# A decoder layer: queries' and keys' kept copies laid out so that one transfer with a repeating source fetches 64 rows, in place of four of 16

## The chip, the cores and the metric

The kernel runs on one core of one Trainium2 chip. A core has five engines with an instruction queue each: TensorE (PE, matrix products; its weight loads are listed as PEld), VectorE (DVE), ScalarE (ACT), GpSimd (POOL) and SyncE (SP), which here only issues DMA transfers. Sixteen DMA engines move data between HBM and the on-chip memory. The metric is the device time of one execution in microseconds (us); lower is better. Several executions are timed and the median is given; one more is recorded by the hardware profiler.

## The reference

One pre-norm decoder layer in float32, for x of shape (4, 1024, 256) and a context of shape (4, 64, 256): layer norm and self-attention with 16 heads of 16 columns, layer norm and cross-attention to the 64 context rows, and a feed-forward block with ternary weights. Shortened:

```python
def attention(x, W_qkv, b_qkv, W_out, b_out):          # B=4, N=1024, E=256, 16 heads, d=16
    q, k, v = split(x @ W_qkv + b_qkv)
    energy = einsum('bqhe,bkhe->bqhk', q, k)           # not scaled before the softmax
    attn = softmax(energy, axis=-1) / sqrt(E)
    return einsum('bihv,bvhd->bihd', attn, v).reshape(B, N, E) @ W_out + b_out

x = x + attention(layernorm(x), ...)
x = x + cross_attention(layernorm(x), ctx, ...)        # 64 context rows, 16 heads, scores / sqrt(16)
x = x + ffn(x)                                         # layernorm(gelu(x @ ternary(W_fc).T)) @ ternary(W_proj).T

def ternary(W):                                        # absmean
    gamma = mean(abs(W)) + 1e-6
    return sign(W / gamma) * minimum(round(abs(W / gamma)), 1)
```

The self-attention scores are large, since they are not scaled and the biases are, so they are computed from a high and a low part of each factor.

## The kernel before, in words

The four sequences are batches b = 0 to 3; the 16 heads of a batch are four groups g of four heads. One group of one batch is a unit, u = 4b + g, and the kernel goes through the 16 units in order.

*Projection.* `project(b, c)` (L348) computes queries and keys of half of the heads of a batch (c = 0: groups 0 and 1; c = 1: groups 2 and 3), in four pieces of 512 columns (tokens): q half 0, k half 0, k half 1, q half 1. A piece is two products of 256 columns on PE (L363); ACT writes each product's high part, rounded to fp32r, into a buffer `hl` (L366), and DVE the low part, which is the product minus its high part (L367). A piece's `hl` has 128 rows (features) by 2 parts by 512 columns. One transfer (L372) then writes it to scratch tensors in HBM, `kept_q` or `kept_k`, of shape (2, 128, 1024): part, feature, token. There are two buffers of the kind `hl`, and other short-lived tiles use them as well (`bv_wide`, `neg`, `lnb_wide`).

*Fetching.* `fetch(u)` (L375) reads the unit's queries and keys back from the scratch tensors. A unit is two pairs of heads, and each pair has a tile q and a tile k of 128 rows by 1024 columns: 64 rows for either head n of the pair. These 64 rows are four blocks of the head's 16 features: q has the parts (high, high, low, low), k has (high, low, high, low), so that one product over 64 rows sums the four products of parts. Each block of 16 rows is a transfer of its own, 64 KB, so a pair needs 16 transfers and a unit 32. Unit 0's are cut into two halves of the columns as well, which makes 64, and eight of those are issued by POOL (`aside`). The tiles q and k have four buffers each, so two units' worth.

*The main loop.* Each unit has 16 steps: two halves of the queries by eight blocks of 128 keys. A step computes the scores of both pairs (PE: a product of k and q, and one of the selection matrix `sel` with the transposed maxima `mT`, which subtracts each row's maximum), their exponentials (ACT, L906: four a step, 128 by 512), and the weighted sum with the values (`weigh`, PE into `ps_acc`). The maxima come from a pass of their own that runs ahead of the scores by 19 of its pieces: `maxima(u)` (L423) has 32 pieces, each two products of q and k (`ps_ring<-k,q`) and two maximum reductions on DVE (`mx`, L445, about 0.68 us each). So a unit's k is first used about at step 6 of the unit before. A planner with due times (`due`, `later`, `aside`) puts other work into the steps: layer norm `ln1(b)`, the projections and values of coming batches, the context's side, the cross-attention `post(b)` of batches that are done, and from unit 13 on the ternary weights. All of it shares a ring of seven PSUM banks; an eighth bank holds the weighted sums.

*Order.* PE's and SP's instructions keep the order of the program. Those of DVE, ACT and POOL are placed when the kernel is built, by a scheduler that models durations, except where one is pinned; an engine then runs them strictly in that order. SP issues its transfers in order, too, and each transfer uses one of eight semaphores in turn: it waits for the landing of the one eight before it.

*What else SP issues near the fetches.* Unit 1's fetch is followed by the load of batch 1's rows (`x<-in_x`, 1 MB), by the context's weights and biases (`late_loads`, L776, which has the loads of `wo` and `xwo`: 32 KB each, 32 rows of 1 KB, read as 2 x 16 rows). Unit 2's fetch, in the first two steps of unit 1, is followed by batch 2's rows. Unit 14's and unit 15's fetches are followed by the loads of the raw weights of the feed-forward block (`raw<-in_wfc`, `raw<-in_wproj`, 1 MB each); DVE first sums their absolute values (`part<-raw`, L735). Layer norm begins with statistics of the loaded rows on DVE (`bn<-x`, L241).

In before's fetch, one head's 64 rows are read by

```python
for i, part in enumerate(order):                      # (0, 0, 1, 1) for q, (0, 1, 0, 1) for k
    r, f = 64 * n + 16 * i, f0 + 16 * n
    issue(out=t[r : r + 16, cols].bitcast(F32), in_=kept[part, f : f + 16, cols])
```

Of the kernel before, what the change touches and what calls it, by code (L numbers as in the profile page):

```python
# [9 lines left out]
F32 = mybir.dt.float32  # L10
# [7 lines left out]
B, S, E = 4, 1024, 256  # L18
H, D = 16, 16
SK = 64  # L20
HID = 1024
P = 128
# [8 lines left out]
def decoder_layer(ctx, tc, a, out):  # L31
# [15 lines left out]
    nc = tc.nc  # L47
# [14 lines left out]
    def dma(**kwargs):  # L62
        ordered(nc.sync.dma_start(**kwargs))
# [38 lines left out]
    for name in ("wq", "wk"):  # L102
# [5 lines left out]
        t = const.tile([P, E // P, H, D], F32, name=name)  # L108
# [4 lines left out]
    for name in ("bq", "bk"):  # L113

        t = const.tile([P, 2], F32, name=f"{name}_c")
        for g in range(NG):
            r = 64 * (g % 2)
            dma(
                out=t[r : r + 64, g // 2 : g // 2 + 1],
                in_=a[name].rearrange("(j e) g -> g j e", e=32)[g, :, 1 : 1 + D],  # L120
# [35 lines left out]
    dram = main_stack.enter_context(tc.tile_pool(name="dram", bufs=1, space=DRAM))  # L156
# [4 lines left out]
    for i in range(3):  # L161
        t = (const if i else main).tile([P, NT, VW], F32, tag=f"v_sb{i}", name=f"v_sb{i}")
# [28 lines left out]
    def bank():  # L191
        return ps[state["banks"]]()
# [4 lines left out]
    def product(out, terms, start=True, stop=True):  # L197

        n = len(terms)
        strips = [slice(32 * j, 32 * j + 32) for j in range(4)] if state["split"] else [slice(0, P)]  # L200
        for i, (lhsT, rhs) in enumerate(terms):
            for r in strips:
                matmul(
                    out[r, :], lhsT=lhsT[:, r], rhs=rhs, start=start and i == 0,
                    stop=stop and i == n - 1,
                )
# [122 lines left out]
    xnT_of, qk_of, split_of, m_of, pieces_of = {}, {}, {}, {}, {}  # L329

    def ln1(b):
        mv = main.tile([P, NT, 2], F32, tag="mv1", name="mv1", bufs=2)
        rs = main.tile([P, NT], F32, tag="rs1", name="rs1", bufs=2)
        xnT_of[b] = xnT = main.tile([P, 2, S], F32, tag="xnT", name="xnT")
        n = NT if state["split"] else NT // 2
        for i0 in range(0, NT, n):
            for i in range(i0, i0 + n, 2):
                yield "free"
                ln_stats(main, mv, [(i + k, b * NT + i + k) for k in range(2)])
            yield "free"  # L340
            ln_rstd(main, rs[:, i0 : i0 + n], mv[:, i0 : i0 + n, :])
            for i in range(i0, i0 + n, 4):
                yield "free"
                xn = ln_normalised(post_pool, mv, rs, i, b * NT + i, 4)
                yield "rows"
                ln_transposed(xnT[:, :, i * P : (i + 4) * P], xn)

    def project(b, c):  # L348

        split_of[b, c] = [  # L350
            dram.tile([2, P, S], F32, tag=f"kept_{name}", name=f"kept_{name}", bufs=6) for name in "qk"
        ]
        first = (b, c) == (0, 0)

        for side, half in ((0, 0), (1, 0), (1, 1), (0, 1)):
            w, bias = (wq, wk)[side], bqk[("bq", "bk")[side]][:, c : c + 1]
            hl = main.tile([P, 2, 512], F32, tag="exp" if first and half else "hl", name="hl", bufs=4 if first and half else 2)
            width = 256 if state["split"] else 512
            for i0 in range(0, 512, width):
                yield "cols+"  # L360
                cols, part = slice(half * 512 + i0, half * 512 + i0 + width), slice(i0, i0 + width)
                pq = bank()[:, 0:width]
                product(  # L363
                    pq, [(w[:, i, c * P : (c + 1) * P], xnT_of[b][:, i, cols]) for i in range(2)]
                )
                nc.scalar.activation(hl[:, 0, part].bitcast(F32R), pq, AF.Identity, bias=bias)  # L366
                nc.vector.scalar_tensor_tensor(  # L367
                    hl[:, 1, part], pq, bias, hl[:, 0, part], ALU.add, ALU.subtract
                )
            cols = slice(half * 512, (half + 1) * 512)  # L370
            issue = nc.scalar.dma_start if first and (side or half) else dma
            issue(out=split_of[b, c][side][:, :, cols].rearrange("l p t -> p l t"), in_=hl)  # L372
            pieces_of[b, c] = pieces_of.get((b, c), 0) + 1

    def fetch(u):  # L375

        b, g = divmod(u, NG)
        pairs = qk_of[u] = []
        rest = []
        for pair in range(2):  # L380
            q = main.tile([P, S], F32R, tag="q", name="q", bufs=4)
            k = main.tile([P, S], F32R, tag="k", name="k", bufs=4)
            pairs.append((q, k))
            kept_q, kept_k = split_of[b, g // 2]
            f0 = 64 * (g % 2) + 32 * pair

            def parts(t, kept, order, n, cols, issue, f0=f0):
                for i, part in enumerate(order):
                    r, f = 64 * n + 16 * i, f0 + 16 * n
                    issue(out=t[r : r + 16, cols].bitcast(F32), in_=kept[part, f : f + 16, cols])  # L390

            if u:
                halves = (slice(0, S),)
            else:
                halves = (slice(0, 512), slice(512, S))
            for n in range(2):
                parts(q, kept_q, (0, 0, 1, 1), n, halves[0], dma)
            for cols in halves:
                for n in range(2):

                    aside = u == 0 and pair == 1 and n == 0
                    parts(k, kept_k, (0, 1, 0, 1), n, cols, nc.gpsimd.dma_start if aside else dma)
            for n in range(2):
                for cols in halves[1:]:
                    rest.append((parts, q, kept_q, (0, 0, 1, 1), n, cols, dma))
            if pair:
                for f, *args in rest:
                    f(*args)
            yield
# [278 lines left out]
    due, later, aside = Line(), Line(), Line()  # L688
# [141 lines left out]


    first, parts = ln1(0), project(0, 0)
    for _ in range(10):
        next(first)
# [3 lines left out]
    run(parts)  # L838
    state.update(split=True, pinned=False)
    run(fetch(0))  # L840

    sel_f = post_pool.tile([P, 2, P], F32, tag="xn", name="sel_f", bufs=2)
    nc.gpsimd.memset(sel_f, 0.0)
    sel = main.tile([P, 2, P], F32R, name="sel")
    for pair in range(2):

        for n in range(2):
            c = 64 * n + 2 * pair
# [17 lines left out]


    parts = project(0, 1)
    for _ in range(5):
        next(parts)  # L870
# [11 lines left out]
    run(turning.popleft())  # L882
    due.credit = 0.0
    run(fetch(1))
    load_x(1)
    loading = late_loads()
# [22 lines left out]
    for u in range(NU):  # L909
        b, g = divmod(u, NG)  # L910
# [4 lines left out]
        if g == 0:  # L915
            if b == 0:
                later.add(context(), 6)
                later.add(value_bias(), 1)

            for n in ((1, 2), (), (3,), ())[b]:  # L920
                if n > 2:
                    load_x(n)
                due.add(ln1(n), 2)
                due.add(project(n, 0), 8)
                due.add(values(n), 8)
                if n == 1:
                    due.add(project(n, 1), 8)
            if b % 2:

                due.add(project(b // 2 + 2, 1), 8)  # L930
            if b == B - 1:
                load_x(0, view=x_kept, slot=1)
# [4 lines left out]
        for step in range(2 * NT):  # L937
# [3 lines left out]
            if step < 2 and 0 < u < NU - 1:  # L941
                if step == 0:
                    while pieces_of.get(divmod((u + 1) // 2, NG // 2)) != 4:
                        due.step()
                    fetching = fetch(u + 1)
                next(fetching)
# [152 lines left out]
    halves = 2 * B  # L1099
# [3 lines left out]
    tag = later.tag  # L1103
    while tag is not None or narrows:
        turn += 1
        if tag is not None and turn % 5 in (0, 2):
            exps += "Exp" in tag
            tag = next(last, None)
            continue
        sources = []  # L1110
        if wides:
            i = halves - len(wides)
# [72 lines left out]
```

## Time and profile before

| | before |
|---|---|
| median of 3 executions | 1333.93 us (1332.51 to 1334.63) |
| the profiled execution | 1333.76 us |
| its span, first to last instruction | 1331.7 us |
| TensorE clock granted, mean | 0.977 |
| PE busy | 1251.0 us, 94% |
| DVE busy | 1041.5 us, 78% |
| ACT busy | 841.5 us, 63% |
| POOL busy | 98.3 us, 7% |
| transfers q<-kept_q on SP | 240 of 64 KB, and those of unit 0 |
| transfers k<-kept_k on SP | 240 of 64 KB, and those of unit 0 |
| bytes by the queue that SP feeds | 68.73 MB, 16.4% of 16 engines' span |

Busy times are shares of the whole span. In a timeline each line has the start, the length, the engine, the source line, the operation, what it writes and reads, how many instructions the line stands for, and in brackets how long the engine stood idle before it and what ended that. "DMA k<-kept_k" in the chain or the waits means that something waited for that transfer to land. A row of a window has the length, the busy time of PE, PEld, DVE, ACT and POOL with the number of instructions, PE's granted clock as a share of full speed, the DMA engines' mean busy share and the data rate in GB/s.

### The profile page before, as it was taken

The numbers are of one execution on the slowest core, as the hardware profiler recorded it, in microseconds if no ns is written. First come the engines' busy times: TensorE is split into PE (matmuls) and PEld (weight loads), VectorE is DVE, ScalarE is ACT, GpSimd is POOL, SyncE is SP. The second block draws the span as 40 slices with busy tenths as digits, with TensorE's granted clock in tenths as the row PEclk, the third lists the DMA queues.
The fourth block names the chain that finished last, engine by engine and source line by source line (L and its number), as shares of the span: only waits on it lengthen the run. The fifth ranks groups of instructions, "written<-read, shape, count | busy, mean of one in ns | idle before, by whom it ended". The sixth has DMA issues, their size and how long they took to land.

```text
span 1331.7 us, 26027 instructions
## 1 busy us (share of the span) xinstructions
PE 1251.0 (94%) x10296; PEld 689.1 (52%) x10296; DVE 1041.5 (78%) x2054; ACT 841.5 (63%) x1557; POOL 98.3 (7%) x138
## 2 busy tenths in 40 slices
PE   5889999989999999989999999999999989999887
PEld 2345544434545454444554544545455457576777
DVE  5888877747878888988788878878989578665865
ACT  2276676636586666677676666576666756645655
POOL 5000000004010000011000000010000100000000
PEclk9889999969999999999999999999999999999989
DMA  5442221201121202040202012212110010100000
GB/s 171 122 139 70 90 68 62 80 32 55 59 66 31 64 2 64 11 118 17 80 21 76 21 45 80 65 62 83 50 47 1 1 64 8 57 0 33 1 32 33
DMA packets 46570, 72.63 MB, mean 55 GB/s; under 512 B 11536, under 2 KB 28176, under 8 KB 46448
## 3 DMA queue, kind: packets, MB, share of 16 engines
q1 hardware_dynamic: 45232, 68.73, 16.4%
q8 instruction: 81, 1.33, 0.4%
q10 hardware_dynamic: 816, 1.57, 0.3%
q0 software_dynamic: 400, 0.66, 0.3%
q14 instruction: 41, 0.34, 0.1%
HBM read 46.81 MB, written 24.12 MB: 53 GB/s over the span
## 4 chain that ended last, share of the span: by engine, by line
PE 70%; DVE 18%; ACT 7%; issue 2%; DMA 1%; POOL 0%; SPq 0%; DVEq 0%; ACTq 0%
PE ps_ring L57 41%; PE ps_acc L57 15%; DVE mx L445 9%; PE ps_wide L57 8%; PE ps_misc L57 3%; ACT exp L906 3%; DVE nm L596 2%; PE ps_misc L60 2%; ACT xn L258 1%; PE ps_ring L60 1%; DMA x<-in_x 1%; ACT L247 1%; DVE bn L241 1%; DVE oT L305 1%; DVE bnh L1023 1%
## 5 line engine op out<-in xcount | busy, mean ns | idle before, releaser
L445 DVE TENSOR_REDUCE mx<-ps_ring 128x1 f32<-128x512 f32 x1024 | 640.4, 679 | 121.5 <-PE ps_ring L57 121.0
L906 ACT ACTIVATE exp<-ps_ring 128x512 f32<-128x512 f32 x1024 | 542.9, 606 | 228.6 <-PE ps_ring L57 228.1
L57 PE MATMUL ps_ring<-k,q 64*128 64x512 f32 x1024 | 273.2, 426 | 18.9 <-DMA k<-kept_k 5.9
L57 PE MATMUL ps_acc<-exp,v_sb 128*32 128x512 f32 x2048 | 278.5, 613 | 0.7 <-ACT exp L906 0.6
L57 PE MATMUL ps_ring<-q,k 64*128 64x512 f32 x1024 | 261.4, 468 | 8.3 <-ACT exp L906 4.9
L57 PE MATMUL ps_ring<-mT,sel 64*128 64x512 f32 x1024 | 221.5, 399 | 0.2 <-ACT mT L463 0.2
L57 PEld LDWEIGHTS ps_ring<-q,k 64*128 64x128 f32 x1024 | 110.0, 185 | 189.7 <-DVE mx L445 67.8
L57 PEld LDWEIGHTS ps_ring<-k,q 64*128 64x128 f32 x1024 | 132.7, 186 | 106.1 <-ACT exp L906 45.9
L57 PEld LDWEIGHTS ps_ring<-mT,sel 64*128 64x128 f32 x1024 | 105.2, 187 | 7.3 <-ACT mT L463 0.7
L57 PEld LDWEIGHTS ps_acc<-exp,v_sb 128*32 128x32 f32 x2048 | 40.9, 108 | 71.2 <-issue 62.8
L309 POOL TENSOR_TENSOR mix<-oT,r 128x256 f32<-128x256 f32 x32 | 20.3, 635 | 658.6 <-DVE r L308 658.6
L1020 ACT ACTIVATE h<-ps_wide 128x1024 f32<-128x1024 f32 x32 | 32.7, 1026 | 46.8 <-PE ps_wide L57 46.6
L57 PE MATMUL ps_wide<-wfc,xl 128*128 128x512 f32 x128 | 54.4, 425 | 5.7 <-DVE xl L281 4.1
L1023 DVE BATCH_NORM_STATS2 bnh<-h 128x6 f32<-128x512 f32 x64 | 40.9, 678 | 21.8 <-ACT h L1020 21.7
L57 PE MATMUL ps_wide<-wproj,hl 128*128 128x256 f32 x256 | 47.2, 308 | 11.4 <-DVE hl L1055 11.4
L1055 DVE SCALAR_TENSOR_TENSOR hl<-ps_misc,lnw,hT 128x512 fp32r<-128x512 f32 x64 | 46.6, 735 | 13.6 <-ACT hT L1054 13.6
L1054 ACT ACTIVATE hT<-ps_misc,lnw 128x512 fp32r<-128x512 f32 x64 | 42.7, 689 | 20.8 <-PE ps_misc L60 20.8
L57 PE MATMUL ps_wide<-wfc,xh 128*128 128x512 f32 x128 | 51.8, 405 | 0.0
L57 PEld LDWEIGHTS ps_wide<-wproj,hl 128*128 128x128 f32 x256 | 35.8, 196 | 16.0 <-DVE hl L1055 13.4
L241 DVE BATCH_NORM_STATS2 bn<-x 128x6 f32<-128x256 f32 x96 | 38.9, 415 | 6.1 <-DMA x<-in_x 4.6
L309 POOL TENSOR_TENSOR mixx<-oT,r 128x256 f32<-128x256 f32 x32 | 20.3, 633 | 309.9 <-DVE r L308 309.9
L57 PE MATMUL ps_wide<-wproj,hT 128*128 128x256 f32 x256 | 41.6, 285 | 0.0
(154 smaller groups left out, 1385.2 us busy)
## 6 DMA issues: line engine op xcount, KB each, us to landing
q<-kept_q SPq DMA_DIRECT2D x240, 64.0 KB
k<-kept_k SPq DMA_DIRECT2D x240, 64.0 KB
kept_q<-hl SPq DMA_DIRECT2D x15, 512.0 KB
kept_k<-hl SPq DMA_DIRECT2D x14, 512.0 KB
out<-x SPq DMA_DIRECT2D x16, 256.0 KB
x<-in_x SPq DMA_DIRECT2D x3, 1024.0 KB
x_kept<-x SPq DMA_DIRECT2D x3, 1024.0 KB
x<-x_kept SPq DMA_DIRECT2D x3, 1024.0 KB
```

The costliest lines, as they stand in the source:

```text
L57: ordered(nc.tensor.matmul(*args, **kwargs))
L60: ordered(nc.tensor.transpose(*args))
L241: pinned(nc.vector.bn_stats(out=st, in_=xs(t)[:, 0, :]))
L247: nc.scalar.activation(sd, mv[:, :, 1], AF.Sqrt, bias=eps_t[:, 0:1])
L309: nc.gpsimd.tensor_tensor(mix[:, :, q * D : (q + 1) * D], heads[:, :, 1 : 1 + D], r.to_broadcast([P, 16, D]), ALU.mult,)
L445: nc.vector.tensor_reduce(mx[:, t, 2 * pair + n : 2 * pair + n + 1, kh], pm, AX.X, ALU.max)
L596: nc.vector.tensor_reduce(nm[:, t, s, :], pm[s].rearrange("p (h k) -> p h k", k=SK), AX.X, ALU.max, negate=True,)
L906: nc.scalar.activation(ex[:, n, :], pe[n], AF.Exp)
L1020: nc.scalar.activation(h[:, t, :], ph.rearrange("p a f -> p (a f)"), AF.Gelu)
L1023: nc.vector.bn_stats(out=st[:, half, :], in_=h[:, t, half * 512 : (half + 1) * 512])
L1054: nc.scalar.activation(hT, pt, AF.Copy, scale=w)
L1055: nc.vector.scalar_tensor_tensor(hl, pt, w, hT.bitcast(F32), ALU.mult, ALU.subtract)
```

## The change

The scratch tensors get another layout, and the fetch of 64 rows becomes one transfer whose source reads the same 32 rows of HBM twice.

- `kept_k` becomes (256, 1024), with the two parts of a feature in neighbouring rows (high of feature 0, low of feature 0, high of feature 1, ...). It is still written by one transfer for each piece. A head's 32 rows in it lie together; the fetch reads them all, and then all of them again: source pattern (2, 32, columns), the outer dimension with step zero.
- `kept_q` becomes (256, 1024), where each head has 16 rows of high parts and then 16 rows of low parts. A piece is written by two transfers, one for the high part, which need not wait for DVE, and one for the low part. The fetch reads each row twice running: source pattern (32, 2, columns), the middle dimension with step zero.
- The 64 rows of q so hold high and low by row: each feature's high part twice, then each low part twice; the 64 rows of k hold high and low by turns, twice. Paired row by row they still give the four products of parts of each feature.
- A unit has eight transfers of 256 KB on SP, in place of 32 of 64 KB; unit 0 has 16, all on SP. POOL issues none of them.

```diff
         split_of[b, c] = [
-            dram.tile([2, P, S], F32, tag=f"kept_{name}", name=f"kept_{name}", bufs=6) for name in "qk"
+            dram.tile([2 * P, S], F32, tag=f"kept_{name}", name=f"kept_{name}", bufs=6) for name in "qk"
         ]
...
-            issue(out=split_of[b, c][side][:, :, cols].rearrange("l p t -> p l t"), in_=hl)
+            kept = split_of[b, c][side][:, cols]
+            if side:
+                issue(out=kept.rearrange("(p l) t -> p l t", l=2), in_=hl)
+            else:
+                kept = kept.rearrange("(g l p) t -> l g p t", l=2, p=D)
+                for part in range(2):
+                    issue(out=kept[part], in_=hl[:, part, :])
...
-            def parts(t, kept, order, n, cols, issue, f0=f0):
-                for i, part in enumerate(order):
-                    r, f = 64 * n + 16 * i, f0 + 16 * n
-                    issue(out=t[r : r + 16, cols].bitcast(F32), in_=kept[part, f : f + 16, cols])
+            def parts(t, kept, n, cols, f0=f0):
+                f = 2 * (f0 + 16 * n)
+                src = kept[f : f + 32, cols]
+                shape = [2, 32, cols.stop - cols.start]
+                if kept is kept_k:
+                    src = src.rearrange("(o r) t -> o r t", o=1).to_broadcast(shape)
+                else:
+                    shape[0:2] = 32, 2
+                    src = src.rearrange("(r o) t -> r o t", o=1).to_broadcast(shape)
+                dma(out=t[64 * n : 64 * n + 64, cols].bitcast(F32), in_=src)
...
             for n in range(2):
-                parts(q, kept_q, (0, 0, 1, 1), n, halves[0], dma)
+                parts(q, kept_q, n, halves[0])
             for cols in halves:
                 for n in range(2):
-
-                    aside = u == 0 and pair == 1 and n == 0
-                    parts(k, kept_k, (0, 1, 0, 1), n, cols, nc.gpsimd.dma_start if aside else dma)
+                    parts(k, kept_k, n, cols)
```

More of the change, by code (lines that the diff above doesn't have):

```diff
@@ L385, in fetch @@
             f0 = 64 * (g % 2) + 32 * pair
-            def parts(t, kept, order, n, cols, issue, f0=f0):
-                for i, part in enumerate(order):
-                    r, f = 64 * n + 16 * i, f0 + 16 * n
-                    issue(out=t[r : r + 16, cols].bitcast(F32), in_=kept[part, f : f + 16, cols])
[L392 to L395, printed above, removed]
+            def parts(t, kept, n, cols, f0=f0):
[8 more added lines that the diff above has]
+                dma(out=t[64 * n : 64 * n + 64, cols].bitcast(F32), in_=src)
+            halves = (slice(0, S),) if u else (slice(0, 512), slice(512, S))
             for n in range(2):
-                parts(q, kept_q, (0, 0, 1, 1), n, halves[0], dma)
+                parts(q, kept_q, n, halves[0])
             for cols in halves:
                 for n in range(2):
-                    aside = u == 0 and pair == 1 and n == 0
-                    parts(k, kept_k, (0, 1, 0, 1), n, cols, nc.gpsimd.dma_start if aside else dma)
-            for n in range(2):
-                for cols in halves[1:]:
-                    rest.append((parts, q, kept_q, (0, 0, 1, 1), n, cols, dma))
+                    parts(k, kept_k, n, cols)
+            rest += [(parts, q, kept_q, n, cols) for n in range(2) for cols in halves[1:]]
             if pair:
```

## The prediction

> **What bounds the kernel now.** I read the page's busy times and slices first, then the waits, then the timelines of SP, ACT and DVE around each transfer that the change touches, and last the windows of the DMA engines.
>
> ```profile
> PE 1251.0 (94%) x10296; PEld 689.1 (52%) x10296; DVE 1041.5 (78%) x2054; ACT 841.5 (63%) x1557; POOL 98.3 (7%) x138
> PEclk9889999969999999999999999999999999999989
> q1 hardware_dynamic: 45232, 68.73, 16.4%
> ...
> PE 70%; DVE 18%; ACT 7%; issue 2%; DMA 1%; POOL 0%; SPq 0%; DVEq 0%; ACTq 0%
> ```
>
> PE is the bound: 94% busy and 70% of the chain that ended last. DMA is 1% of that chain, so quicker fetches have little to win. Among all waits of PE only one names a fetch (columns: total us, times, longest):
>
> ```profile
> PE ps_ring L57 <- DMA k<-kept_k: 5.9, 2, 5.4
> ```
>
> It lies in the start. A steady fetch has slack: unit 2's is issued like this,
>
> ```profile
> 121.90 4.06 SPq L63 DMA_DIRECT2D q<-kept_q  x8
> 126.00 4.96 SPq L63 DMA_DIRECT2D k<-kept_k  x8
> 131.06 3.60 SPq L63 DMA_DIRECT2D q<-kept_q  x8
> 134.99 3.93 SPq L63 DMA_DIRECT2D k<-kept_k  x8
> 139.02 0.38 SPq L63 DMA_DIRECT2D kept_k<-hl  x1
> 139.44 0.47 SPq L63 DMA_DIRECT2D x<-in_x  x1
> ```
>
> and over the units PE first uses pair 0 27 to 31 us after the fetch starts, pair 1 31 to 36 us after it (least: unit 14, 24.0 and 28.4). What else is not PE's peak is a few bubbles. Two matter here: PE idle from 83.2 to 87.6 us, while DVE does x's statistics (bn, from 81.44) in one burst, and 261 to 300 us:
>
> ```profile
> 283.75 1.08 ACT L906 ACTIVATE exp<-ps_ring 128x512 f32<-128x512 f32 x2 [1.09 <-PE ps_ring L57]
> 284.72 0.84 ACT L366 ACTIVATE hl<-ps_ring,bk_c 128x256 fp32r<-128x256 f32 x2
> 290.50 1.08 ACT L906 ACTIVATE exp<-ps_ring 128x512 f32<-128x512 f32 x2 [4.93 <-PE ps_ring L57]
> ```
>
> The window of 275 to 300 us (length, then busy time of PE, PEld, DVE, ACT, POOL with counts, PE's clock, DMA share, GB/s):
>
> ```profile
> 275.00:300.00 25.00, 22.29 (x118) 8.98 (x117) 10.54 (x19) 8.40 (x19) 0.63 (x1) 0.61 0.11 42
> ```
>
> PE's product for that first hl was at 256.30, but ACT evicts it at 284.72: the ring's banks are held for 28 us, and the clock falls to 0.61. Seven steps with a fill of other work take 44.6 us (257.27 to 301.85) against 7 x 3.76 = 26.3 at the usual pace of such a step, so 18.3 us are lost.
>
> **What the changed fetch costs on the DMA engines.** This decides the case. Before has no transfer whose source repeats; the question is what an outer dimension of two does. It does have transfers whose outer dimension is two: the loads of xwo, 32 rows of 1 KB read as (2, 16, 256). Alone on the queue from 86.5 to 94 us, windows show (last two columns as above)
>
> ```profile
> 88.00:90.00 2.00, 2.00 (x10) 0.48 (x9) 2.00 (x6) 1.98 (x4) 0.00 (x0) 0.50 0.14 47
> 90.00:92.00 2.00, 1.71 (x8) 0.83 (x6) 0.21 (x2) 1.99 (x5) 0.00 (x0) 0.50 0.14 45
> ```
>
> A share of 0.14 is about 2 of 16 engines (0.125), and one xwo follows another every 0.736 us: 16 rows one after another at the 46 ns of a 1-KB row. With outer dimensions of 128 the same queue had 0.99 and 370 GB/s (23 to 26 us). So I take it that a transfer is cut along its slowest dimension, and that k's new source (2, 32, columns) puts 64 rows on two engines, 32 on each. q's source (32, 2, columns) still spreads over 16, and the writes of kept_q (8, 16, 512) go to 8. One k transfer of 64 rows of 4 KB then takes 32 x 156 ns (the row time of 4 KB in the quiet fetches) = 5.0 us, in unit 0, with 2 KB at 84 ns, 2.7. A unit has four: 20.0, and four of q's with 4 rows each per engine, 4 x 0.62 = 2.5: 22.5, taken as 22.7 with its gaps, and 1.5 us from issue to the first rows: 24.2 us, in place of 15 to 17. That is still ahead of pair 1's first use (28.4 at the least) and pair 0 is there by half of it. So steady PE work loses nothing by the fetch itself. But engines 0 and 1 now work through some 20 us of rows, SP issues all in 4 us (8 x 0.46 in place of 32), and whatever it issues behind them waits there: a load that spreads over 16 engines lands when its last two do.
>
> The Trainium skill speaks against this change in the same direction: "DMA: Bandwidth & Descriptors", section "Rules for kernel authors", says that a leading zero-stride repeat of c copies confines the whole transfer to at most c engines. By it k is on two engines, as I take from xwo's rows; without it (16 engines) the sum would be rival A's.
>
> **The sum, part by part.** The built order of instructions shows PE's order unchanged; SP's 24 removed issues per unit (and POOL's eight in unit 0) cost nothing now, as SP's queue is idle most of the time. But that order also puts DVE's first use of each load earlier, right where a short fetch would have it ready; DVE works in order, so a late load stops the maxima (679 ns each) behind it, the seven banks fill and PE stops within about 1 us (two maxima banks a step of 2.9 to 3.76). PE has no slack to catch up, and each stop costs a stretch of half clock as at 86.35 to 93.2 (6.9 us, 3.4 lost); I take 3. So a stall of s costs s - 1 + 3.
>
> 1. Start. Unit 0's chain before:
>
> ```profile
> 31.33 2.77 DMA k<-kept_k
> ...
> 34.34 3.39 PE ps_ring L57 x19
> 37.73 18.03 DVE mx L445 x30
> ```
>
> k comes at 32.95 and 34.10 and the reduces run to 55.77. After, eight k transfers at 2.7 (21.5) and eight of q at 0.34 (2.7) follow one another on the two engines from about 29: first at 33.2, second 36, last at 53.2. Eight reduces of 0.60 need that last one: 53.2 + 4.8 = 58.0 against 55.77: **+2** (bounds -1, if DVE catches up on alternate halves, and +5, at the 173 to 251 ns that a contended 4-KB row took).
> 2. Batch 1's x (issued 68.31, landed 75.6). Behind unit 0's k (53.2), the two kept writes (2.7 + 1.3) and unit 1's fetch (22.7) engines 0 and 1 reach it at 79.9; its 1 MB took from 2.9 (wfc's rows) to 7.3 us (issue to landing): lands at about 84.5. DVE's bn now stands behind the 50th maximum, 71.1 in before's time, 73.2 with step 1: a stall of 11.3 - 1 + 3 = 13.3. The old bubble there (83 to 95 us, 7.3 lost) goes, but about 3 of it stays, as ACT and DVE still have the same statistics and xn to do: -4.3. **+9**.
> 3. Batch 2's x (issued 139.44). Engines 0, 1 are free at 121.9 + 24.2 = 146.1, a kept write and 1 MB follow (5.6): 151.7. DVE wants it at 139.85 (before: 155.21): 11.9 - 1 + 3, less 1.2 of the burst that no longer falls later: **+12.7**.
> 4. Project (2, 0), the bubble at 261 to 300. In the built order ACT evicts each hl at once, so that bubble's 18.3 go. In its place ACT's eviction of k0 needs the only free hl buffer, whose two kept_q writes stand behind unit 4's fetch: 241.8 + 24.2 + 2.7, and 0.4 = 269.1, ACT is there at 257.4: 11.7 - 1 + 3 = 13.7. **-4.6** (bounds: -17 when the writes pass; +3 if the wait repeats for a later piece), and -0.7 for two pieces that were 4 and 6 exps late near 208 and 218.
> 5. wfc (raw, issued 911.22). Engines free at 894.0 + 24.2, plus 2.9: 921; its first part reduction is wanted at 908.3 (before: 925): 12.8 - 1 + 3 - 0.8: **+14**.
> 6. wproj likewise: 952.45 + 24.2 + 2.9 = 979.6, wanted 969.9: **+12**.
>
> Sum +2 + 9 + 12.7 - 4.6 - 0.7 + 14 + 12.2 = +45. The profiled run took 1333.76 us (span 1331.7 and 2.06 around it), 0.17 below the median of 1333.93, so I add to the median: **1379 us**.
>
> What the trace does not show, with bounds: the half clock per stall is 0 (PE idles too short for it) to 3.4, taken 3 of five stalls: -15 to +2. The slack is 0 to 3.76 (a whole step): -14 to +5. Loads that do not wait for all rows before them, or DVE places that move: -12 each at most.
>
> **Rivals.** A: the repeat does not confine, k spreads over 16 engines like q's. For it: the change's k transfers could be cut along rows of the destination (64), and xwo's could have had another reason. Against: the windows above. Then the fetch is as short as 256 KB x 8 at 300 GB/s, the loads are early, and only gains stay: start -4.4 (k 5 us sooner after kept_k at 27.55), the burst at 83 to 95 -3, project (2, 0) -17, late pieces -0.7: -25, **1309 us**. It decides if a k transfer takes under about 1 us of rows on an engine. This is the case on the other side.
> B: k on two engines, but loads pass or the stalls are half absorbed (DVE's in-order wait hits a stretch where PE has other work): +2 + 5 + 6 - 10 + 6 + 6 = +15, about **1349**. For it: PE has scores and weigh products of its own between two maxima; against: the maxima stand in PE's written order in each step.
> C: rows are slower than 156 ns. At 173 a unit takes 25 us, at 251 36 us, past pair 1's first use (28.4 to 36): each of 14 units then waits some 3 us: +42 on top, **1420**. It decides at about 180 to 200 ns. Against: only two engines work, others' rows do not crowd them.
>
> **How the numbers follow.** Chances: forecast (1360 to 1400) 0.55; B (1337 to 1360) 0.19; C (over 1400) 0.09; A (below 1331) 0.14; within 0.2% (2.7 us, about what a measurement tells from no change) 0.03, if the stalls and project (2, 0) happen to balance. Slower is 0.55 + 0.19 + 0.09 = 0.83. The range that leaves 2 in 10 out: 1338 to 1402. The forecast's own: 1360 to 1400.
>
> **What would show it.** Right: k transfers landing about 5 us apart, DMA share near 0.13 in the 20 us after each fetch; DVE waiting for x near 73 and 140 us and for raw near 908 and 970, 10 to 13 us each; ACT waiting near 257 for kept_q; no wait of PE for k past unit 0; PEclk low in those slices. Wrong: a share of 0.5 or more during fetches (A); no idle DVE at the loads (B); "PE ps_ring <- DMA k" many times (C).

## The result and the profile after

The changed kernel took 1409.23 us (median of 4, 1405.58 to 1409.82), the kernel before beside it 1333.22 us (median of 4, 1328.2 to 1334.63). The ratio is 1.0569, 95% interval 1.054 to 1.0598: slower by 76 us. The forecast was 1379, with a range to 1402; the direction and the place of the loss were right, its size was not.

The page of the changed kernel, busy times and the first line of the DMA queues, then the shares of the chain that ended last:

```profile
PE 1248.5 (89%) x10296; PEld 686.1 (49%) x10296; DVE 1042.2 (74%) x2054; ACT 840.7 (60%) x1557; POOL 94.4 (7%) x130
...
q1 hardware_dynamic: 38008, 68.97, 15.6%
...
PE 61%; DVE 16%; DMA 13%; ACT 7%; issue 2%; SPq 1%; POOL 0%; DVEq 0%; ACTq 0%
```

Busy times are those of before within 4 us, so no engine has more to do. The same bytes take no larger share of the DMA engines. But DMA was 1% of the chain and is now 13%. Which transfers, the waits of the changed kernel tell (total us, times, longest):

```profile
DVE bn L241 <- DMA x<-in_x: 31.4, 4, 17.6
...
DVE part L740 <- DMA raw<-in_wfc: 19.2, 1, 19.2
DVE part L740 <- DMA raw<-in_wproj: 17.0, 1, 17.0
ACT hl L366 <- DMA kept_q<-hl: 16.8, 2, 15.9
PE ps_ring L57 <- DMA k<-kept_k: 12.6, 3, 8.3
```

The first three are loads that the change does not touch, the fourth is a write that it only splits in two; SP issues all of them behind a fetch. k itself keeps PE waiting only in unit 0. In the kernel before, no line of the waits names raw, and DVE's for x are short:

```profile
DVE bn L241 <- DMA x<-in_x: 4.6, 3, 2.8
```

SP's timeline of the changed kernel around unit 2's fetch:

```profile
137.13 1.44 SPq L63 DMA_DIRECT2D q<-kept_q  x2
138.62 1.12 SPq L63 DMA_DIRECT2D k<-kept_k  x2
139.84 1.18 SPq L63 DMA_DIRECT2D q<-kept_q  x2
141.06 1.05 SPq L63 DMA_DIRECT2D k<-kept_k  x2
148.75 3.92 SPq L63 DMA_DIRECT2D kept_k<-hl  x1
152.71 2.47 SPq L63 DMA_DIRECT2D x<-in_x  x1
```

SP has issued the whole fetch in 5 us, where it took 17 (over units 1 to 15 it now takes 4.7 to 13.0). By the times at which the trace's semaphores count, the four transfers of k then land at 149.60, 154.67, 163.45 and 168.54. Each k has one count about 0.4 us after SP has issued it and then two, up to 0.9 us apart, which I read as one for each of two DMA engines; a q has sixteen, a write of kept_q one and then eight. x, issued at 152.71, lands at 172.47, 4 us behind the last k. In between the windows of the changed kernel show two engines' worth of work, 0.125 of sixteen being two (length; busy time of PE, PEld, DVE, ACT, POOL; PE's clock; DMA share; GB/s):

```profile
147.00:152.00 5.00, 5.00 (x57) 2.62 (x48) 4.02 (x8) 3.02 (x6) 0.00 (x0) 1.00 0.14 52
...
162.00:167.00 5.00, 0.00 (x0) 0.00 (x0) 0.00 (x0) 0.00 (x0) 0.00 (x0) 0.50 0.13 52
```

In the second window every engine stands still. DVE's and PE's timelines of the changed kernel say why; the brackets hold the idle time before the line and what ended it:

```profile
152.40 2.47 DVE L450 TENSOR_REDUCE mx<-ps_ring 128x1 f32<-128x512 f32 x4
172.49 0.75 DVE L241 BATCH_NORM_STATS2 bn<-x 128x6 f32<-128x256 f32 x2 [17.62 <-DMA x<-in_x]
```

```profile
156.43 0.39 PE L57 MATMUL ps_ring<-mT,sel 64*128 64x512 f32 x2
174.47 0.80 PE L57 MATMUL ps_ring<-k,q 64*128 64x512 f32 x2 [17.65 <-DVE hl L367]
```

DVE has x's statistics next in its order and waits; it has done the last maximum at 154.87 and PE, with no bank left, stops at 156.82 for 17.65 us. Both lose about the same time, at each late load: DVE's waits at the four are 9.45, 17.62, 19.2 and 17.0 us, PE's stops there 9.5, 17.65, 18.6 and 17.1. Where the time went, by the start times of the same maximum reductions in both traces (after minus before, differences between stretches):

| stretch | forecast, us | measured, us |
|---|---|---|
| start, unit 0's maxima | +2 | +7.6 |
| batch 1's x | +9 | +7.4 |
| batch 2's x | +12.7 | +19.4 |
| two late pieces near 208, 218 us | -0.7 | -1.0 |
| last pieces of the project before (2, 0) | none | +4.9 |
| project (2, 0) | -4.6 | +0.1 |
| wfc | +14 | +19.6 |
| wproj | +12.2 | +18.5 |
| all the rest | 0 | -0.6 |
| sum | +45 | +75.9 |

75.9 is the difference of the two spans, 1407.6 and 1331.7.

### The profile page after: what moved, and what is told of

Its sections match the earlier page's. It is cut to its first block, busy times and chain, and to the rows that moved or that the text cites. A ratio compares the mean times of both kernels' runs of the same rounds, so it can differ in the third digit from the quotient of the medians.

```text
span 1407.6 us, 25564 instructions
## 1 busy us (share of the span) xinstructions
PE 1248.5 (89%) x10296; PEld 686.1 (49%) x10296; DVE 1042.2 (74%) x2054; ACT 840.7 (60%) x1557; POOL 94.4 (7%) x130
## 4 chain that ended last, share of the span: by engine, by line
PE 61%; DVE 16%; DMA 13%; ACT 7%; issue 2%; SPq 1%; POOL 0%; DVEq 0%; ACTq 0%
PE ps_ring L57 34%; PE ps_acc L57 13%; PE ps_wide L57 7%; DVE mx L450 7%; DMA x<-in_x 4%; PE ps_misc L57 3%; DMA kept_k<-hl 2%; DVE nm L601 2%; ACT exp L911 2%; PE ps_misc L60 2%; DMA raw<-in_wproj 2%; DMA k<-kept_k 2%; DMA raw<-in_wfc 2%; DMA kept_q<-hl 2%; SPq L63 1%
## 5 line engine op out<-in xcount | busy, mean ns | idle before, releaser
L57 PE MATMUL ps_ring<-k,q 64*128 64x512 f32 x1024 | 267.9, 429 | 60.0 <-DVE hl L367 42.1
L57 PE MATMUL ps_ring<-q,k 64*128 64x512 f32 x1024 | 262.4, 469 | 29.0 <-DVE x L324 17.1
L241 DVE BATCH_NORM_STATS2 bn<-x 128x6 f32<-128x256 f32 x96 | 38.8, 415 | 32.8 <-DMA x<-in_x 31.4
L57 PE MATMUL ps_wide<-wproj,hl 128*128 128x256 f32 x256 | 46.7, 305 | 11.4 <-DVE hl L1060 11.4
L422 ACT COPY v_sb<-ps_ring 128x256 f32<-128x256 f32 x32 | 12.0, 376 | 69.8 <-PE ps_ring L57 69.8
L57 PE MATMUL ps_ring<-kx,q 64*128 64x256 f32 x192 | 29.0, 392 | 18.6 <-DVE mx L450 18.6
L366 ACT ACTIVATE hl<-ps_ring,bk_c 128x256 fp32r<-128x256 f32 (+1 forms) x30 | 14.6, 489 | 49.6 <-PE ps_ring L57 32.2
```

The lines of the kernel that those rows point to most:

```text
L57: ordered(nc.tensor.matmul(*args, **kwargs))
L241: pinned(nc.vector.bn_stats(out=st, in_=xs(t)[:, 0, :]))
```

## The experiments

**Two engines, or the new layouts?** The first kernel differs from the changed one only in that a head's rows of k come by two plain transfers.

```diff
                 if kept is kept_k:
-                    src = src.rearrange("(o r) t -> o r t", o=1).to_broadcast(shape)
+                    for r in (64 * n, 64 * n + 32):
+                        dma(out=t[r : r + 32, cols].bitcast(F32), in_=src)
+                    return
```

> The changed kernel with one difference: a head's 64 rows of k come by two transfers of 32 rows with no repeat (source 32 x columns), in place of one whose outer dimension of two is the repeat; layouts, writes and q's fetch stay. Theory (an outer dimension of two puts a transfer on two DMA engines, and DVE and ACT then stand behind the loads and writes queued on those two): each k transfer completes with 16 counts, a unit's fetch takes 10 us or less from first issue to last landing in place of 23 to 32, the waits of DVE for x (17.6 and 9.5 us) and for the raw weights (19.2 and 17.0 us) and of ACT for kept_q (15.9 us) are gone, and the old bubble of project (2, 0) does not come back, as the built order evicts at once: 1305 to 1318 us. Rival 1 (the new layouts, kept_q's two writes or q's doubled rows cost the time): 1390 us or more. Rival 2 (only the built order of DVE, which places first uses of loads 10 to 18 maxima earlier, costs the time; it is nearly the same here): 1370 us or more.

1316.7 us, ratio 0.9871 (0.9841 to 0.9902) to the kernel before: 92 us less than the changed kernel, and 1.3% below the kernel before. Its k transfers land with sixteen counts. The windows over its unit 2's fetch:

```profile
119.00:123.00 4.00, 4.00 (x48) 2.06 (x44) 2.89 (x6) 2.66 (x6) 0.00 (x0) 1.00 1.05 259
123.00:127.00 4.00, 3.95 (x40) 1.74 (x36) 3.97 (x9) 2.06 (x4) 0.64 (x1) 1.00 1.04 236
```

All sixteen engines are busy (a share slightly over 1 comes from rows that overlap a window's edge) and the fetch is over 12 us after its first issue (117.47 to 129.43), a little more than the 10 expected. Of the waits of PE, ACT and DVE for a DMA, none for a load is over 3 us:

```profile
ACT hl L366 <- DMA kept_k<-hl: 5.8, 2, 3.8
PE ps_ring L57 <- DMA k<-kept_k: 5.2, 2, 3.0
...
DVE bn L241 <- DMA x<-in_x: 4.7, 3, 2.7
```

Layouts, kept_q's two writes and q's doubled rows are in it as in the changed kernel, so none of these cost the time (rival 1 falls). Its built order has DVE's uses of the loads (x of batches 1 and 2, wfc, wproj) within 4 maxima of the changed kernel's, so that early order alone doesn't cost it either (rival 2 falls): it needs a load that is late.

**The repeat, or the outer dimension of two?** In k32 both are gone. The next kernel brings back the dimension without the repeat.

```diff
-            dram.tile([2 * P, S], F32, tag=f"kept_{name}", name=f"kept_{name}", bufs=6) for name in "qk"
+            dram.tile([2 * P * (1 + (name == "k")), S], F32, tag=f"kept_{name}", name=f"kept_{name}", bufs=6)
+            for name in "qk"
...
-                issue(out=kept.rearrange("(p l) t -> p l t", l=2), in_=hl)
+                kept = kept.rearrange("(o p l) t -> o p l t", o=2, l=2)
+                for o in range(2):
+                    issue(out=kept[o], in_=hl)
...
+                if kept is kept_k:
+                    src = kept.rearrange("(o r) t -> o r t", o=2)[:, f : f + 32, cols]
```

> The changed kernel, but each piece of k is written to two copies far apart in the scratch tensor, and the fetch reads one copy and then the other: source (2, 32, columns) as in the changed kernel, but the outer dimension has a real step and nothing is read twice. Theory (the outer dimension of two decides, not the repeat): k transfers complete with two counts, about 5.1 us apart, and the time is the changed kernel's plus a little for 14 further writes of 512 KB, 1405 to 1425 us. Rival (a step of zero, or reading the same rows twice, is what is slow): the fetch takes about 10 us and the time is 1305 to 1325 us.

1413.14 us, ratio 1.0591 (1.0564 to 1.0619). A window inside unit 7's fetch, and then two waits for loads, of this kernel:

```profile
500.00:504.00 4.00, 4.00 (x32) 1.65 (x28) 3.76 (x8) 2.84 (x6) 0.64 (x1) 1.00 0.13 51
```

```profile
DVE bn L241 <- DMA x<-in_x: 34.9, 5, 17.3
...
DVE part L744 <- DMA raw<-in_wfc: 19.9, 1, 19.9
```

Again two counts at the landing of each k, and those of that fetch land at 503.50, 508.59, 514.90 and 520.03. Reading the same rows twice is not what is slow: it is the outermost dimension of two, repeated or not.

**What is queued behind the fetch.** The fetch is left at two engines; batch 1's and 2's rows are loaded ahead of it.

```diff
-    run(fetch(1))
     load_x(1)
+    run(fetch(1))
...
-            if u == 1 and step == 2:
+            if u == 1 and step == 0:
                 load_x(2)
```

> The changed kernel with batch 1's and batch 2's rows loaded ahead of the fetch that they followed, the two-engine fetch unchanged, and the raw weights' loads still behind theirs. Theory (what is queued behind the fetch loses the time, not the fetch): the two stalls of DVE for x go (8 and 21 us lost), the start, project (2, 0) and the two raw loads stay: 1375 to 1388 us. Rival (PE or DVE wait for k itself, which comes as late or later): 1405 us or more.

1386.38 us, ratio 1.039 (1.0355 to 1.0424): 23 us below the changed kernel and inside the expectation. The longest wait for x is 5.0 us, and DVE waits for both raw loads as in the changed kernel:

```profile
DVE part L740 <- DMA raw<-in_wfc: 20.6, 1, 20.6
ACT hl L366 <- DMA kept_q<-hl: 17.7, 2, 16.5
DVE part L740 <- DMA raw<-in_wproj: 16.4, 1, 16.4
DVE bn L241 <- DMA x<-in_x: 13.7, 5, 5.0
```

So it is the place in SP's queue, behind the fetch, that makes x late.

**Another queue.** The loads of x and of the raw weights are issued by ACT.

```diff
-            dma(
+            issue = (lambda **k: ordered(nc.scalar.dma_start(**k))) if b in (1, 2) and view is x_view and n == 1 else dma
+            issue(
                 out=x_of[b][:, sl, :], in_=view[:, b * NT + i * step : b * NT + (i + 1) * step, :]
             )
...
-        dma(
+        nc.scalar.dma_start(
             out=flat.rearrange("p (c f) -> p c f", c=w.shape[1]),
```

> The changed kernel with the loads of batch 1's and 2's rows and of both raw weights issued by ACT, on ACT's own queue, in place of SP's; the two-engine fetch stays on SP's. In the built order DVE's first uses stand behind maxima 38, 114 and 870 (50, 118 and 884 in the changed kernel), so a load that is as late as there would cost 4 to 14 us more each. Theory 1 (a load waits in its queue, and a DMA engine takes the rows of two queues by turns): on engines 0 and 1 a 1-KB row of x waits for one 4-KB row of k at most, 64 rows x (162 + 46 ns) = 13 us at worst after the issue; the four waits of DVE, 9.5, 17.6, 19.2 and 17.0 us in the changed kernel, sum to less than 30: 1345 to 1385 us. Theory 2 (an engine works off the rows of all queues in the order of their issue): waits as long as in the changed kernel or longer, 1405 to 1450 us.

1390.87 us, ratio 1.043 (1.0403 to 1.0457): between the two theories. The mechanism of theory 1 shows: batch 2's x, issued at 147.03, lands at 165.71, 5 us before the last k of the fetch that was issued 6 us ahead of it, and from 155 to 165 us the trace has as many 1-KB rows as 4-KB rows, some ten of each in a microsecond. But the time that this takes, 18.7 us, is more than the 13 of the expectation, and DVE asks for x earlier:

```profile
165.74 0.75 DVE L242 BATCH_NORM_STATS2 bn<-x 128x6 f32<-128x256 f32 x2 [15.34 <-DMA x<-in_x]
```

The four waits of DVE sum to 45 us (12.3, 15.3, 1.0 and 16.5) where under 30 were expected. wfc was issued ahead of the fetch here, so its wait went for that reason and tells nothing of the queues.

**k's part alone.** q is kept and fetched as before, k as in the change. (q's rows stand in the old order and k's in the new one, so the rows that meet are not of the same feature and the products are not the reference's; the work is the same.)

```diff
+                if kept is kept_q:
+                    for i in range(4):
+                        r, f = 64 * n + 16 * i, f0 + 16 * n
+                        dma(out=t[r : r + 16, cols].bitcast(F32), in_=kept[i // 2, f : f + 16, cols])
+                    return
```

> Of the change only k's part: k kept with neighbouring parts and fetched by one repeating transfer, q kept, written and fetched as before (four transfers of 16 rows). The built order then has DVE's first uses of the loads where the kernel before has them (behind maxima 62, 134 and 898 in place of 50, 118 and 884). Theory (two engines late, the loss is lateness minus DVE's place): start +5 to +8, x of batch 1 late by 0 to 3 us, of batch 2 by 0 to 6, the raw weights by 2 to 8 each, project (2, 0) as in the changed kernel (15 lost, 18 regained): 1340 to 1365 us. Rival (the lost time does not depend on DVE's places): within 1% of the changed kernel, 1395 us or more.

1421.05 us, ratio 1.0635 (1.0592 to 1.0677): the expectation missed by 56 us, and upward. Three of DVE's four waits are shorter, where its places are later (2.3, 12.0 and 6.3 us for 17.6, 19.2 and 17.0); that for batch 1's x is longer (13.2 for 9.45). And a new wait came, of PE for k in nearly every unit:

```profile
PE ps_ring L57 <- DMA k<-kept_k: 39.2, 14, 7.5
...
DVE bn L241 <- DMA x<-in_x: 19.3, 4, 13.2
...
DVE part L741 <- DMA raw<-in_wfc: 12.0, 1, 12.0
```

SP's timeline of this kernel names the reason:

```profile
147.30 1.08 SPq L63 DMA_DIRECT2D k<-kept_k  x2
148.48 15.75 SPq L63 DMA_DIRECT2D q<-kept_q  x8
164.27 1.04 SPq L63 DMA_DIRECT2D k<-kept_k  x2
```

The seventh of pair 1's eight q transfers needs the semaphore of the first k, eight transfers back, and SP stands until that k has landed (158.05); the eighth waits for the second k (163.91). So pair 1's k is only issued at 164.27 and lands at 179.92, 37 us after the fetch began. In every later unit of this kernel SP stands in the same way. In the changed kernel, with eight transfers a unit, SP stands for a k only in the start, where unit 0 has sixteen. I had counted the two engines' rows, and not the eight semaphores; the run therefore doesn't measure what DVE's later places are worth by themselves.

**Project (2, 0), and why k32 is faster than before.** First the kernel before, with only the small tile bv_wide moved out of the hl buffers.

```diff
-        wide = main.tile([P, 2, P], F32, tag="hl", name="bv_wide", bufs=2)
+        wide = main.tile([P, 2, P], F32, tag="bvw", name="bv_wide")
```

> The kernel before, with one edit: bv_wide (1 KB a partition) gets a buffer of its own instead of one of the two hl buffers. Transfers are as before. The built order then holds project (2, 0)'s evictions back by 12, 8 and 4 exponentials at three pieces in place of 20, 16, 14, 10, 10 and 6 at six. Theory (before's bubble at 261 to 300 us is made by these late evictions, not by transfers): about half of its 18 us come back, 1320 to 1329 us. Rival (that bubble has to do with the 32 small transfers): no change, 1331 us or more.

1320.53 us, ratio 0.9893 (0.9856 to 0.9929), with before's own 32 transfers a unit. Over the maxima from 256 to 272 its trace gains 12.9 us on before's. ACT's timeline of this kernel, around the project, shows k's first piece evicted at once (before: 284.72) and only k's second and what follows it still late:

```profile
259.50 0.47 ACT L366 ACTIVATE hl<-ps_ring,bk_c 128x256 fp32r<-128x256 f32 x1 [1.01 <-PE ps_ring L57]
263.25 0.47 ACT L366 ACTIVATE hl<-ps_ring,bk_c 128x256 fp32r<-128x256 f32 x1 [1.00 <-PE ps_ring L57]
...
279.54 0.84 ACT L366 ACTIVATE hl<-ps_ring,bk_c 128x256 fp32r<-128x256 f32 x2
280.25 0.49 ACT L366 ACTIVATE hl<-ps_ring,bq_c 128x256 fp32r<-128x256 f32 x1
```

The bubble of before thus comes from that small tile in hl's buffers and the order of ACT and DVE that is built around it, and not from the 32 transfers. The same edit on the changed kernel:

> The changed kernel with bv_wide in a buffer of its own; the two-engine fetch stays. Theory (in project (2, 0) ACT waits 15.9 us for an hl buffer whose kept_q write is queued behind the fetch): k's first piece now has a free buffer and only its second needs that one, some 8 us later, so the wait falls to about 8 us: 1397 to 1404 us. Rival (the loss there comes from something else): as the changed kernel, 1407 us or more.

1398.78 us, ratio 1.0483 (1.045 to 1.0517): 10 us less than the changed kernel, as the wait for kept_q goes from 15.9 to 9.9 and comes one piece later:

```profile
309.12 0.47 ACT L366 ACTIVATE hl<-ps_ring,bk_c 128x256 fp32r<-128x256 f32 x1 [9.92 <-DMA kept_q<-hl]
```

Last, two forms of k32. With bv_wide moved:

> The kernel with k fetched by two transfers of 32 rows, and bv_wide in a buffer of its own. The built order then holds back none of project (2, 0)'s evictions (one piece by 4 exponentials without it), and ACT's two waits for kept_k (5.8 us in all) go. Theory: 4 to 6 us below the kernel with 32-row transfers, 1309 to 1314 us. Rival (those waits lie beside PE's work): 1315 to 1319 us.

1313.25 us (median of 6, 1309.45 to 1319.41), ratio 0.9842 (0.9811 to 0.9874). The median is in the expected interval, but the intervals of k32 and this one overlap; in the traces it is 4 us ahead by the end of project (2, 0) (21.9 us before the kernel before, against 17.9). It has the lowest median of all, well below both kernels, but is not told apart from k32. And with k32's two transfers cut into four of 16 rows, as many for k as before:

> As the kernel with k in two transfers of 32 rows, but four of 16 rows each, as many for k as the kernel before has; layouts, kept_q's writes and q's one transfer stay. The built order has DVE's first uses of the loads where the kernel before has them, and holds five pieces of project (2, 0) back by 13, 9, 8, 4 and 4 exponentials. Theory (number and size of the transfers count for nothing as long as all 16 engines share them, only the built order does): no wait for a load, part of the bubble of project (2, 0), 1318 to 1328 us. Rival (fewer and larger transfers were the gain of the 32-row kernel): 1331 us or more.

1325.0 us, ratio 0.9929 (0.99 to 0.9957). That is inside the expectation and below the rival's 1331, but above k32; no load is late. The pieces of project (2, 0) that the order holds back do not account for the distance: over the project itself both gain about the same on the kernel before (k32 11.1 us, from 6.8 ahead to 17.9; this one 11.4, from 0.8 behind to 10.6 ahead). They part earlier, above all at batch 1's x: from unit 0's end to 104 us of before's time k32 gains 3.8 us and this kernel loses 1.5. Its order has x's statistics behind maximum 62, as the kernel before has, and PE stops there as it does in before (83.2 to 87.6 us):

```profile
88.36 1.34 PE L57 MATMUL ps_ring<-k,q 64*128 64x512 f32 x2 [4.37 <-issue]
```

k32's order has them behind maximum 52, and its trace has no such stop of PE. So most of the distance goes with DVE's place in the built order, and only 1.6 us of it with the start. That the number of transfers is what moved that place is likely, as nothing else differs, but how the order came about is not shown.

## Why the prediction was right and wrong

**Right.** That a source of two outer parts goes to two engines, taken from xwo's rows in the profile before, holds: two counts for each k, a share of 0.13 and 51 to 52 GB/s, and kcopies shows that the repeat is not needed for it. The Trainium skill ("DMA: Bandwidth & Descriptors", section "Rules for kernel authors") states it for any outermost dimension of fewer than 16, with a leading repeat as its example; this case agrees, for the repeat (two counts at landing, 52 GB/s) and, in kcopies, without it (51 GB/s). The four stalls of DVE stood where the sum put them, at x of batches 1 and 2 and at both raw weights, with ACT's at project (2, 0). That PE doesn't wait for k in steady units held too, but with less room than forecast, and in part by luck: unit 6's last k lands 0.46 us before PE's first use of it, and the fetch ahead of wfc took 28.6 us, more than the 28.4 after which the kernel before uses that k; it was in time because DVE's wait for wfc had stopped PE. The price of a stall held: 17.6 us of waiting became 19.4 of time, 19.2 became 19.6, 17.0 became 18.5, which is 0.4 to 1.8 over the stall where the sum had 0.8 to 2. Its two terms did not hold singly: PE's stops are not 1 us shorter than DVE's waits (17.65 for 17.62), and what comes on top is less than 3.

**Wrong: the duration of a unit's fetch**, which the prediction put at 24.2 us from 32 rows x 156 ns a transfer. Rows alone on the two engines take 162 ns and a k transfer 5.1 us, as it said. But from its first issue to its last landing a unit's fetch took 27.1 to 31.7 us in the trace: 31.4 for unit 2's, 27.9 for unit 4's, 28.6 and 31.7 for those ahead of wfc and wproj. In unit 2's fetch the median of a 4-KB row, by the microsecond, is 281 to 312 ns from 140 to 144 us, while q's rows run on all engines, and 218 to 351 from 157 to 161, while x's 1-KB rows run on the others; but it is 206 to 262 from 144 to 147 too, when q's rows on the other engines are done. The first k of that fetch, among q's rows, lands 11 us after its issue. So 32 x 156 ns was too little for the first k's of a fetch and for a k beside a load; why rows were slow is shown for neither. With that the loads landed 4 to 7 us later than worked out: DVE waited 17.6, 19.2 and 17.0 us where 11.9, 12.8 and 9.7 were worked out, ACT 15.9 where 11.7 was. (With 9.7, step 6 comes to 10.9 or 11.7 by the prediction's own terms; it says 12 and adds up 12.2.) That is +6.7, +5.6 and +6.3 us on steps 3, 5 and 6 and most of step 4's miss. The prediction had 173 to 251 ns as a contended row and put it aside, with the words "only two engines work, others' rows do not crowd them", under rival C. There the two were tied together: slower rows should have meant PE waiting in each unit. The runs show slower rows without that wait, since a fetch of 27 to 31 us still came in time for pair 1's first use, 30.3 to 35.1 us after the fetch began in units 3 and 5 to 13, and 47 us or more where a stall lay between. Beyond unit 0 the slow rows only reached the loads and writes.

**Mis-sized: step 1, the start**: +7.6 in place of +2. The first k landed at 34.81, not 33.2, and the eight follow one another by 2.99 us on average (34.81 to 55.71), not 2.7; the last came 2.5 us late. Ten reductions, not eight, were still to do behind it, from 57.02 to 63.09 us.

**Wrong: step 4, project (2, 0)**: -4.6 forecast, +0.1 measured. The old bubble went, as forecast, and the new wait took all of it: the kept_q writes land at 309.17 and 310.40, 3 us later in the kernel's own time than worked out.

**Left out:** +4.9 us before project (2, 0). The fetch of unit 3 also stands ahead of a kept_k write (issued 235.27, landed 251.30), and q's piece that reuses the buffer waits for it 3.98 us. The prediction had listed the writes of kept copies behind fetches for project (2, 0) only; here a write took 16 us to land, and the project came back to its buffer before that.

**Step 2, batch 1's x** came out at +7.4 for +9, but two misses nearly cancel in it: the load landed at 88.19, 3.7 us later than worked out, and DVE, held up by the start, asked for it 5.6 us later.

**Rival A**, all sixteen engines, was put at 1309 us; k32 is that case, at 1316.7. By the end of project (2, 0) it is 17.9 us ahead of the kernel before, but only 11.1 of that came in the project, where 17 were forecast; the stretch of batch 1's x gained 3.8, where 3 were, and the start about 1, not 4.4.

## What to carry to other kernels

Look at a transfer's outermost dimension before its size: one transfer in place of four is no gain if it leaves the work to two DMA engines, and its cost then appears at whatever shares those engines behind it, not at its own consumer. On an engine that works in order, a late load stops everything behind it (here 17.6 us of waiting cost 19.4 of time), so check each place where an order was built on the assumption that the load is there. Where a change alters durations that a scheduler sees, compare the built orders first: moving one small tile out of hl's buffers, and with it the order, was worth 13 us in the kernel before.

## What was not expected of the hardware

A 4-KB row of a two-engine transfer took 162 ns in most of the fetch, but 200 ns and more in other stretches, not only beside rows on the other engines: from 553 to 556 us in the changed kernel the DMA share was 0.13, which is two engines, at 34 GB/s and medians of 245 to 309 ns a row, and from 557 on a row took about 162 ns. What sets these slow stretches is open; no run here was made to tell.

Rows of two queues on the same DMA engine are taken by turns (one 1-KB row of 46 ns, one 4-KB row of 162, a pair every 0.20 us, 155 to 165 us in the kernel with loads on ACT's queue). So a second queue passes a long fetch, but row for row: the 1-KB rows get about a quarter of the engine's time.

Some of SP's issues behind a fetch themselves last long: that of kept_q's write at 156.03 in the changed kernel takes 10.47 us, where the same issue took 0.64 at 128.43 and none in the kernel before is over 1.9. The transfer that used its semaphore last had landed at 149.60, so it is not that wait; what it is, no run here shows.
